# Selective scan and mixture of experts under adaptive layer norm, float32: the Newton step on rstd and the gates' low part from GpSimd to Vector, a seventh product with C on GpSimd

## The chip, the cores and the metric

One core of a Trainium2 chip runs the whole kernel in one launch. The metric is device time in microseconds. The engines are called as the profile calls them: PE (TensorE), DVE (VectorE), ACT (ScalarE), POOL (GpSimd) and SP (SyncE, which here only issues DMAs).

## The reference

The input x has 8 batches of 1024 tokens of 256 channels, in float32. Each batch has its own six modulation vectors, a product of `silu(c)` with `wmod`. Two blocks follow each other:

```python
mod = (_silu(L0_c) @ L0_wmod).reshape(L0_c.shape[0], 6, 1, -1)
sa, ca, ga, sb, cb, gb = (mod[:, 0], mod[:, 1], mod[:, 2], mod[:, 3], mod[:, 4], mod[:, 5])
h = _layernorm(x, axis=-1) * (1 + ca) + sa
x = x + ga * _L0_attn_ref(h, ...)      # selective scan
h = _layernorm(x, axis=-1) * (1 + cb) + sb
x = x + gb * _L0_ffn_ref(h, ...)       # mixture of 8 experts, 2 per token
```

In the first block, each of 256 channels has 16 states. `dt = softplus(...)` comes from two small projections of h, `a = exp(dt * A)`, `v = dt * u * B`, and each state runs the recurrence `h = a * h + v` along the 1024 tokens. The output is `y = sum over the 16 states of h * C`, plus `u * D`. In the second block a softmax over 8 experts picks the top two; their outputs are weighed by gates and added.

## The kernel before

**Tiling.** A stage is half a batch: 512 tokens, 256 channels as two tiles of 128 channels by 512 tokens. There are 16 stages, a first and a second half for each batch. The second half starts its scans from values kept from the first (tile `carry`).

**One stage.** For each of the 16 states n: SP loads the rows of B and C, spread over all partitions (`bb`, `cc`). POOL makes `v = du * bb` for both channel tiles at once (L1029, 128x1024). ACT makes `a` in PSUM (L1040), one per channel tile. DVE runs one scan per channel tile (L1051, a in PSUM, v in SBUF). The product with C goes either to DVE, two instructions of 128x512 into `hcD` (L1065), or to POOL, one of 128x1024 into `hs` (L1070). A string for each kind of stage, `C_ENG`, says which, state by state: D or P. PE adds the products up in PSUM, by transposes that accumulate into `y` (L1122). Before the states, POOL makes `du = dt * g` (L968) from ACT's softplus `dt` (L962).

**The back part of a stage** runs during the states of the next one: x + y on DVE (L1158), statistics of the layer norm (L786, L789), the factors of the norm, the norm itself on ACT (L831), transposes on PE (L862), a high and a low part of the result (`hi`, `lo`), the logits, the route (some fifteen small DVE steps, L1250 to L1271), the gates and their high and low parts (`gs`, L1297 and L1300), eight experts on PE (L1340), weighed by ACT (L1418) and summed by PE (L1428). POOL issues the DMA that adds the result to the output (L1501).

**The factors of the norm.** ACT guesses rstd with a logarithm and an exponential (L808 to L811). One Newton step then refines it: five small steps on the SBUF tile `ln` (128 x 8 in the middle stages, since the statistics of x two stages on are taken along), each using the result of the one before (L816 to L820, on POOL).

**Order.** No order is written out by hand. Each operation is given to a planner with its engine, a cost, and a due time `DUE[kind]`, one value per kind and phase; the phases are stage 0, stage 1, the middle stages 2 to 13, stage 14 and stage 15. The planner runs a model of the five engines, always takes the operation due first among those ready or soon ready (`PATIENCE` says how soon, per engine), and so fixes the order on every engine. `RINGS` gives the number of buffers per kind of tile: 4 of `v`, 3 of `hs`, 3 of `a`, 5 of `bb`, for instance. An operation that needs a buffer waits until all users of the one four (three, five) back have ended.

```python
def with_c(s, n):
    return ("hcD" if C_ENG[(0, 0, 2 - stages[s].first, 3, 3)[phase_of(s)]][n] == "D" else "hs", s, n)
```

So the first of the four strings of `C_ENG` is for stages 0 and 1, the second for the first halves among stages 2 to 13 (2, 4, ... 12), the third for their second halves, the fourth for stages 14 and 15.

Of the kernel before, what the change touches and what calls it, by code (L numbers as in the profile page):

```python
# [29 lines left out]
C_ENG = ("DDPDDPDDPDDPDDPD", "DPDDPDPDPDPDPDDD", "DPDPDPDPDPDPDPDD", "DDPDDPDDPDDPDDDD")  # L30
AHEAD = 1668.1
PATIENCE = {"ACT": 0.14, "DVE": 0.13, "PE": 0.25, "POOL": 0.5, "SP": 0.28}
# [5 lines left out]
    "load c": -2243.51,  # L38
    "load wmod0": -2004.07,
    "load wmod1": -1988.48,  # L40
    "load wmod2": -2.06,
    "load wmod3": -1957.81,
    "load W_x": -1.71,
    "load W_dt": -1965.24,
    "load b_dt": -116.61,
    "load A": -369.4,
    "load D": -1656.1,
    "load Wg": -357.62,
    "Wg hi": -1640.08,
    "Wg lo": -1616.04,  # L50
    "c^T": -414.35,
    "exp c": -1984.89,
    "1 + exp c": -351.35,
    "1 / c": -1644.2,
    "silu c": -1648.48,
    "mod1": -29.89,
    "mod1 out": -1640.92,
    "mod1 + 1": -57.77,
    "mod2": -97.07,
    "mod2 out": -2072.57,  # L60
    "mod3": -2117.64,
    "mod3 out": -1963.21,
    "mod3 + 1": -1953.8,
    "ga0": -437.02,
    "ga1": -460.54,
    "ga2": -73.86,
    "ga3": -2623.36,
    "gb0": -1953.35,
    "gb1": -357.52,
    "gb2": -461.1,  # L70
    "gb3": -27.31,
    "ga mod": -63.28,
    "ga mod D": 262.7,
    "1 / ga": -76.35,
    "gb^T": 279.89,
    "gb out": -406.31,
    "gb store": -483.98,
    "W_x^T": -3768.39,
    "W_x out": -436.84,
    "W_dt^T": -374.71,  # L80
    "W_dt out": -436.11,
    "exp A": -369.97,
    "-A": -74.32,
    "be rows": -2072.64,
    "be hi": -98.66,
    "be lo": -1963.34,
    "be": -55.72,
    "eps": -4332.43,
    "gates hi": (-235.79, -2460.72, -339.79, -149.99, -1797.16),
    "gates lo": (-24.1, -2044.84, -2133.06, -343.23, -3860.41),  # L90
    "load be": -15.49,
    "iw": -70.2,
    "load x": (-1989.96, -1978.86, -17.48, 8.4, -7.21),
    "stats1": (-2009.67, -1972.63, -69.27, -86.05, 47.99),
    "aggr1": (-1640.3, -1975.3, -1.3, -91.31, -2296.04),
    "before1": (-107.3, 986.06, -2961.9, -2961.25, -2977.69),
    "rstd1": (-359.36, 14.85, -2578.96, -2707.53, -2572.88),
    "norm1": (-24.76, -3800.78, 53.71, -15.89, -19.88),
    "trans1_0": (-2098.37, 28.07, -3664.64, -2478.96, -2711.13),
    "modg_0": (962.12, -427.57, -16.09, -2517.23, -444.87),  # L100
    "modD_0": (-1969.85, -43.93, -15.26, 0.47, -464.06),
    "trans1_1": (-2098.96, -16.51, -1646.42, -70.34, -17.88),
    "modg_1": (962.68, 28.65, -3869.23, -4.95, -390.32),
    "modD_1": (-16.02, -141.37, -3869.42, -2640.81, -526.1),
    "W_x / ga": (-2440.92, -1341.87, -50.77, -365.17, -1339.66),
    "proj": (-46.32, -3262.07, -1417.18, -7075.25, -1106.5),
    "rows": (-113.21, 892.07, -2147.14, -25.83, -373.01),
    "spill": (-1509.92, -46.65, -82.13, -108.28, -408.55),
    "dt0": (-2836.1, -86.93, -410.11, -472.19, -22.27),
    "softplus0": (8.96, -483.31, -563.94, -2696.95, -430.27),  # L110
    "dt1": (-2436.14, 985.9, -367.41, -1987.69, -75.38),
    "softplus1": (-3763.28, -2241.26, -2842.46, -2274.94, -367.03),
    "du": (-486.18, -2239.99, -70.63, -2154.13, -1629.08),
    "load B": (-1369.55, -17.6, -22.69, -296.42, -29.81),
    "load C": (-0.98, -16.67, 9.77, -2484.98, -15.04),
    "v": (-499.25, -85.1, -76.35, -47.8, 21.22),
    "a0": (-416.33, -341.56, -12.06, -392.16, -398.23),
    "a1": (-2633.56, -2630.9, -2268.36, -376.87, -2271.91),
    "scan0": (-345.29, -130, -84.13, -483.71, 835.51),
    "keep0": (-2622.16, -2801.29, -2480.02, -431.11, -2842.99),  # L120
    "C0": (-421.59, -408.48, -2258.73, -2296.35, -21.24),
    "scan1": (-350.22, -136.94, -86.02, -2760.06, -4.38),
    "keep1": (-2229.92, -335.27, -2547.2, -437.52, -439.8),
    "C1": (-414.5, -73.48, -2299.69, -2313.25, -19.25),
    "C": (-493.68, -127.22, -2167.24, -2223.87, 18.97),
    "y D": (19.24, -476.83, -54.5, -465.41, -8.25),
    "y": (-2254.19, -1637.88, -9.88, -1109.95, -3.56),
    "y C": (-473.82, -1635.95, -9.36, -7.82, 0.38),
    "load We": 4.3,
    "We hi": 992.95,  # L130
    "We lo": -499.19,
    "x + y": (-2642.38, -4495.38, -2303.57, -15.13, 893),
    "store x": (-2250.83, -2697.53, -2498.03, -14.55, -4714.94),
    "stats2": (-456.02, -1616.02, -2198.38, 0.86, -442.22),
    "aggr2": (-1761.59, -1623.66, -1485.56, 4.02, -32.11),
    "before2": (-53.78, -586.98, -7.88, 277.95, -2145.97),
    "rstd2": (-1659.97, -76.28, -71.01, -1965.28, -301.08),
    "norm2": (-15.76, -2440.99, -2156.75, 21.3, -62.97),
    "trans2_0": (-427.62, -2364.93, -1608.28, -17.84, 261.41),
    "hi0": (-2629.72, -4055.61, -4630.1, -3019.49, -2113.5),  # L140
    "mod2_0": (-343.91, -1615.01, -2238.87, -947.94, -35.03),
    "lo0": (-1317.6, -80.15, -2289.65, -464.16, 16.03),
    "trans2_1": (-3111.61, -1780.04, -10.03, -2604.76, 261.39),
    "hi1": (-2600.7, -738.55, -2256.02, 51.68, -2142.05),
    "mod2_1": (-359.16, -1823.24, -2242.34, -2256.16, 65.08),
    "lo1": (-2347.63, -3887.63, -77.67, -574.96, -1738.61),
    "logits^T": (-86.05, 0.71, -4.18, 0.12, 26.21),
    "logits out": (-2084.24, -89.2, -2470.09, -2118.52, -71.72),
    "logits": (-589.23, -70.63, -1938.4, -18.59, -408.58),
    "route": (-2625.88, -2360.01, -3907.92, -64.39, -2292.96),  # L150
    "gates": (-133.28, -75.36, -3858.04, -2448.11, -2203.07),
    "gates^T": (-2898.97, -1962.73, -2234.43, -4003.16, 6.19),
    "gates out": (-85.21, -9.58, -616.13, -18.22, -363.26),
    "biases": (-1642.72, -1.18, 6.14, 4.55, -932.33),
    "expert0": (-1632.13, -334.88, 2.48, 0.74, 28.86),
    "weigh0": (-2623.2, -2251.01, -2465.87, -2251.67, -3291.15),
    "sum0": (-1630.65, -2.35, 6.77, 2.59, 343.88),
    "gb": (-6.16, -2002.75, -2252.74, -1770.24, -2231.99),
    "turn": (13.97, 2.84, 5.77, -17.42, 288.49),
    "out": (-2240.75, -63.84, -406.3, -1777.56, -2456.12),  # L160
    "expert1": (-89.29, -20.09, 1.79, 275.85, 64.81),
    "weigh1": (-5.26, -122.87, -2272.08, -2165.17, -179.06),
    "sum1": (-5.22, -8.29, 3.93, 280.73, -101.5),
    "store": (-32.73, -46.88, -15.77, 11.83, -2124.92),
    "load gb": (-1904.24, -1904.24, -1904.24, -1904.24, -2839.22),
    "last bias": -92.62,
    "last": -2205.05,
    "last expert": 307.58,
    "last store": -16.76,
# [252 lines left out]
def kernel(  # L422
# [358 lines left out]
    def statistics(i, s, t, part, st, o):  # L781

        x, k0, tg, n_ = ("x", s), part[0], part[1] - part[0], str(i)

        def stats(k):
            nc.vector.bn_stats(new("st", st, [P, 2 * TG, 8])[:, o + k, 0:6], T[x][:, k0 + k, :])  # L786

        def aggr(k):
            nc.vector.bn_aggr(T[st][:, o + k, 6:8], T[st][:, o + k, 0:6])  # L789

        for k in range(tg):
            plan.add(
                "stats" + n_, "DVE", 0.33 if i == 2 else 0.39, t, lambda k=k: stats(k), r=[x + ((k0 + k) // 2,)],
                w=[st + (o + k,)], ring=("st", st),
            )
        for k in range(tg):
            plan.add("aggr" + n_, "DVE", 0.09, t, lambda k=k: aggr(k), w=[st + (o + k,)])

    def factors(i, t, st, ln, n):
# [13 lines left out]
        def newton():  # L813

            r, m, v, tt = row(0), row(1), row(2), nc.gpsimd.tensor_tensor
            tt(m, r, r, ALU.mult)  # L816
            tt(m, m, v, ALU.mult)
            nc.gpsimd.tensor_scalar(m, m, -0.5, 1.5, ALU.mult, ALU.add)
            tt(r, r, m, ALU.mult)
            tt(m, row(3), r, ALU.mult)  # L820
# [4 lines left out]
        plan.add("rstd" + n_, "POOL", 0.95 + 0.055 * n, t, newton, r=[st], w=[ln])  # L825
# [323 lines left out]
    def back(s, t, part):  # L1149
# [164 lines left out]
        for i in (0, 2):  # L1314
            plan.add("gates hi", "ACT", 0.18, t, lambda i=i: gates_hi(i), r=[G], w=[gs + (i,)], ring=("gs", gs))
# [247 lines left out]
```

## Time and profile before

| what | value |
|---|---|
| median of 3 runs | 1039.54 us (1039.06 to 1041.3) |
| the profiled execution: its time, its span | 1040.26 us, 1038.5 us |
| busy: PE, DVE, ACT, POOL | 928.7, 959.8, 845.7, 918.5 us |
| 255 v products on POOL (L1029) | 605.8 us, 2404 ns each |
| 96 C products on POOL (L1070) | 229.9 us, 2396 ns each |
| 320 C products on DVE (L1065) | 214.2 us, 684 ns each |
| 19 Newton steps of five on POOL (L816 to L820) | 0.20 us per instruction |
| 17 low parts of the gates on POOL (L1300) | 4.7 us, 279 ns each |
| granted TensorE clock, mean | 0.962 |

Durations are of one profiled execution. An instruction's duration runs from its start to its end, including time in which it has begun but is held up. Instructions that follow each other on DVE overlap a little, so what one costs its queue is the time from start to start: 0.61 us for a C product on DVE, for instance. Lines in the profile have the form: line, engine, operation, what it writes <- what it reads, shapes, count, then busy time and mean duration, then idle time before it and what ended most of that.

### The profile page before, as it was taken

How to read it: one execution, taken by the hardware profiler on the slowest of the kernel's cores; microseconds unless marked ns; L12 is line 12 of the kernel's file. 1: busy time of each engine (PE TensorE's matmuls, PEld its weight loads, DVE VectorE, ACT ScalarE, POOL GpSimd, SP SyncE). 2: the span in 40 equal slices, each digit the busy share in tenths (PEclk: the TensorE clock that was granted, in tenths of full speed). 3: DMA queues.
4: the chain of work that ended last, by engine and by line, in shares of the span. 5: the costliest groups of instructions: out<-in, count | busy, mean ns of one | idle time of the engine just before them, and what ended most of it. 6: DMA issues, size and time to landing. Idle time of an engine off the chain costs nothing. (4 is left out here: it accounts for less than half of the span.)

```text
span 1038.5 us, 17114 instructions
## 1 busy us (share of the span) xinstructions
PE 928.7 (89%) x5525; PEld 739.9 (71%) x5525; DVE 959.8 (92%) x1488; ACT 845.7 (81%) x1845; POOL 918.5 (88%) x515
## 2 busy tenths in 40 slices
PE   6656798798899989999999989999998998999998
PEld 4444676586676868687777868688686867778886
DVE  3798999999999999999999999999999998999947
ACT  5855678889699988988899988988898986988661
POOL 4999879999999999999999999999999997988600
PEclk9657998899899999999999999999999999999999
DMA  6556327375655647475665737475575637656102
GB/s 203 185 182 219 122 88 234 96 209 147 194 157 156 208 108 211 113 217 155 166 221 146 219 85 212 123 209 175 138 240 128 221 67 204 169 148 198 39 6 46
DMA packets 103865, 165.20 MB, mean 159 GB/s; under 512 B 10160, under 2 KB 37216, under 8 KB 103776
## 3 DMA queue, kind: packets, MB, share of 16 engines
q1 hardware_dynamic: 95728, 156.22, 49.4%
q0 software_dynamic: 8048, 7.89, 5.1%
q8 instruction: 44, 0.72, 0.3%
q14 instruction: 45, 0.37, 0.1%
HBM read 146.76 MB, written 17.31 MB: 158 GB/s over the span
## 5 line engine op out<-in xcount | busy, mean ns | idle before, releaser
L1029 POOL TENSOR_TENSOR v<-du,bb 128x1024 f32<-128x1024 f32 x255 | 605.8, 2404 | 17.8 <-DMA bb<-bcd 11.7
L1040 ACT ACTIVATE a<-dt,negA 128x512 f32<-128x512 f32 x512 | 348.5, 697 | 52.9 <-DVE hcD L1065 33.0
L1070 POOL TENSOR_TENSOR hs<-hs,cc 128x1024 f32<-128x1024 f32 x96 | 229.9, 2396 | 17.1 <-issue 8.7
L1065 DVE TENSOR_TENSOR hcD<-a,cc 128x512 f32<-128x512 f32 x320 | 214.2, 684 | 13.9 <-ACT carry L1057 7.0
L1418 ACT ACTIVATE wt<-pe,G 128x256 f32<-128x256 f32 x480 | 201.6, 474 | 18.5 <-PE pe L1340 16.8
L1122 PE MATMUL y<-ident,hcD 128*128 128x128 f32 x1280 | 183.3, 285 | 34.8 <-DVE hcD L1065 34.6
L1051 DVE TENSOR_TENSOR_SCAN a<-a,v 128x512 f32<-128x512 f32 x166 | 195.6, 1213 | 8.5 <-POOL v L1029 4.8
L1051 DVE TENSOR_TENSOR_SCAN a<-a,carry,v 128x512 f32<-128x512 f32 x154 | 196.2, 1277 | 1.4 <-POOL v L1029 0.7
L1122 PEld LDWEIGHTS y<-ident,hcD 128*128 128x128 f32 x1280 | 153.8, 147 | 58.0 <-DVE hcD L1065 44.2
L1340 PE MATMUL pe<-we_hi,hi 128*128 128x512 f32 x512 | 179.2, 431 | 7.3 <-ACT wt L1418 4.3
L1340 PE MATMUL pe<-we_lo,hi 128*128 128x512 f32 x512 | 160.7, 395 | 0.0
L1340 PE MATMUL pe<-we_hi,lo 128*128 128x512 f32 x512 | 160.5, 395 | 0.0
L1428 PE MATMUL ma<-ident,wt 128*128 128x128 f32 x960 | 135.8, 275 | 1.2 <-ACT wt L1418 1.2
L1122 PE MATMUL y<-ident,hs 128*128 128x128 f32 x768 | 109.7, 285 | 24.2 <-POOL hs L1070 23.9
L1051 DVE TENSOR_TENSOR_SCAN hs<-a,carry,v 128x512 f32<-128x512 f32 x102 | 125.2, 1266 | 0.0
L1428 PEld LDWEIGHTS ma<-ident,wt 128*128 128x128 f32 x960 | 112.1, 141 | 16.2 <-ACT wt L1418 2.0
L1122 PEld LDWEIGHTS y<-ident,hs 128*128 128x128 f32 x768 | 92.1, 146 | 37.4 <-POOL hs L1070 31.1
L1340 PEld LDWEIGHTS pe<-we_lo,hi 128*128 128x128 f32 x512 | 96.3, 188 | 22.9
L1340 PEld LDWEIGHTS pe<-we_hi,lo 128*128 128x128 f32 x512 | 96.1, 188 | 23.1
L1051 DVE TENSOR_TENSOR_SCAN hs<-a,v 128x512 f32<-128x512 f32 x90 | 106.3, 1208 | 0.0
L1340 PEld LDWEIGHTS pe<-we_hi,hi 128*128 128x128 f32 x512 | 81.5, 190 | 25.6 <-ACT wt L1418 9.2
L831 ACT ACTIVATE xn<-x,ln 128x256 f32<-128x256 f32 x128 | 72.0, 599 | 3.0 <-POOL ln L820 3.0
(134 smaller groups left out, 936.9 us busy)
## 6 DMA issues: line engine op xcount, KB each, us to landing
bb<-bcd SPq DMA_DIRECT2D x256, 256.0 KB, 5.5
cc<-bcd SPq DMA_DIRECT2D x256, 256.0 KB, 5.2
x<-in_L_attn_u_dram SPq DMA_DIRECT2D x16, 512.0 KB, 3.7
out_dram<-x SPq DMA_DIRECT2D x15, 512.0 KB, 3.4
out_dram<-of POOLq DMA_DIRECT2D x15, 512.0 KB, 12.1
wf<-in_L_ffn_We_dram SPq DMA_DIRECT2D x8, 256.0 KB, 4.1
wm<-in_L_wmod_dram SPq DMA_DIRECT2D x2, 512.0 KB
bcd<-xd SPq DMA_DIRECT2D x32, 32.0 KB, 1.6
```

Source lines behind the costliest of these rows:

```text
L831: nc.scalar.activation(new("xn", xn, [P, TG, D])[:, k, :], T[x][:, k0 + k, :], AF.Identity, bias=T[ln][:, 1, o + k : o + k + 1], scale=T[l ...
L1029: nc.gpsimd.tensor_tensor(new("v", v, [P, DC, CL])[:, :, :cl], T["du", s][:, :, :cl], both(T[bb][:, :cl]), ALU.mult,)
L1040: nc.scalar.activation(new("a", a + (j,), [P, CL])[:, :cl], T["dt", s][:, j, :cl], AF.Exp, scale=negA[:, j, n : n + 1],)
L1051: nc.vector.tensor_tensor_scan(part(j), T[a + (j,)][:, :cl], T[v][:, j, :cl], init, ALU.mult, ALU.add)
L1065: nc.vector.tensor_tensor(new("hcD", hc, [P, DC, CL])[:, j, :cl], part(j), T[cc][:, :cl], ALU.mult)
L1070: nc.gpsimd.tensor_tensor(o, o, both(T[cc][:, :cl]), ALU.mult)
L1122: nc.tensor.matmul(new("y", y, [P, 2, D])[:, k % 2, j * P : (j + 1) * P], T[src][:, j, k * P : (k + 1) * P], ident, is_transpose=True, sta ...
L1340: nc.tensor.matmul(pe, T[v][:, j, k * P : (k + 1) * P], w[:, j, 2 * q : 2 * q + 2, :].rearrange("p e d -> p (e d)"), start=n == 0, stop=n ...
L1418: nc.scalar.activation(new("wt", wt, [P, 2, D])[:, i, :], T["pe", s, part, q, k][:, i * D : (i + 1) * D], AF.Copy, scale=T[G][:, k, e : e ...
L1428: nc.tensor.matmul(o[:, j, (k % 2) * P : (k % 2 + 1) * P], T["wt", s, q, k][:, i, j * P : (j + 1) * P], ident, is_transpose=True, start=Fa ...
```

## The change

The five Newton steps go from POOL to DVE, and so does the low part of the gates. The second string of `C_ENG` changes from six products with C on POOL to seven; the third had seven already. Two orders on PE are fixed by added dependencies: the transposes of the first norm and the D part of y go in the order of the stages. Some costs that the planner is given are changed, as are `AHEAD`, `PATIENCE` and all of `DUE`, so that the order on every engine is planned anew.

```diff
-C_ENG = ("DDPDDPDDPDDPDDPD", "DPDDPDPDPDPDPDDD", "DPDPDPDPDPDPDPDD", "DDPDDPDDPDDPDDDD")
-AHEAD = 1668.1
-PATIENCE = {"ACT": 0.14, "DVE": 0.13, "PE": 0.25, "POOL": 0.5, "SP": 0.28}
+C_ENG = ("DDPDDPDDPDDPDDPD", "DPDPDPDPDPDPDPDD", "DPDPDPDPDPDPDPDD", "DDPDDPDDPDDPDDDD")
+AHEAD = 2063.23
+PATIENCE = {"ACT": 0.15, "DVE": 0.22, "PE": 0.22, "POOL": 0.21, "SP": 1.43}
...
         def newton():
 
-            r, m, v, tt = row(0), row(1), row(2), nc.gpsimd.tensor_tensor
+            r, m, v, tt = row(0), row(1), row(2), nc.vector.tensor_tensor
             tt(m, r, r, ALU.mult)
             tt(m, m, v, ALU.mult)
-            nc.gpsimd.tensor_scalar(m, m, -0.5, 1.5, ALU.mult, ALU.add)
+            nc.vector.tensor_scalar(m, m, -0.5, 1.5, ALU.mult, ALU.add)
             tt(r, r, m, ALU.mult)
             tt(m, row(3), r, ALU.mult)
...
-        plan.add("rstd" + n_, "POOL", 0.95 + 0.055 * n, t, newton, r=[st], w=[ln])
+        plan.add("rstd" + n_, "DVE", 0.4, t, newton, r=[st], w=[ln])
...
         plan.add(
-            f"trans{i}_{j}", "PE", (0.13 if i == 1 else 0.11) * tg, t, f, r=[xn + (k,) for k in range(tg)], w=[pt],
+            f"trans{i}_{j}", "PE", (0.15 if i == 1 else 0.12) * tg, t, f, r=[xn + (k,) for k in range(tg)] + ([("t1", s - 1)] if i == 1 and s else []),
+            w=[pt] + ([("t1", s, j)] if i == 1 else []),
...
             plan.add(
-                "y D", "PE", 0.22 * len(tiles), t, lambda: more(gd), r=[gd], w=[y], ring=("y", y)
+                "y D", "PE", 0.22 * len(tiles), t, lambda: more(gd), r=[gd] + ([("yd", s - 1)] if s else []),
+                w=[y, ("yd", s)], ring=("y", y)
             )
...
         def gates_lo():
-            nc.gpsimd.tensor_tensor(
+            nc.vector.tensor_tensor(
                 T[gs][:, :tg, 1], T[G][:, :tg], T[gs][:, :tg, 0].bitcast(F32), ALU.subtract
             )
...
-        plan.add("gates lo", "POOL", 0.22, t, gates_lo, r=[G, gs + (0,)], w=[gs + (1,)], ring=("gs", gs))
+        plan.add("gates lo", "DVE", 0.1, t, gates_lo, r=[G, gs + (0,)], w=[gs + (1,)], ring=("gs", gs))
...
```

In the new order, as the built program has it, Newton stands on DVE in stages 3 to 13 between the two scans of state 4 (in second halves behind the first C product of that state too), and the low part of the gates between the two scans of state 11 in nearly all of these stages. On POOL the order from a stage's start is v0, v1, v2, v3, v4 and C1 (in either order), v5, the store of an earlier stage's result, v6, C3, v7, v8.

## The prediction, made before the changed kernel ran

> **What bounds the kernel now.** I read the page's busy times first, then windows, to see in which stretch which engine is full.
>
> ```profile
> PE 928.7 (89%) x5525; PEld 739.9 (71%) x5525; DVE 959.8 (92%) x1488; ACT 845.7 (81%) x1845; POOL 918.5 (88%) x515
> ```
>
> ```profile
> 195.00:845.00 650.00, 609.48 (x3758) 486.97 (x3756) 632.72 (x947) 573.96 (x1246) 633.34 (x336) 0.99 0.59 170
> 845.00:975.00 130.00, 124.64 (x757) 99.78 (x755) 119.36 (x173) 109.56 (x244) 110.28 (x60) 1.00 0.54 151
> 975.00:1038.50 63.50, 58.32 (x324) 47.21 (x322) 41.94 (x99) 27.86 (x74) 8.68 (x16) 0.98 0.16 28
> ```
>
> The columns after the length are PE, PEld, DVE, ACT and POOL busy. From 195 to 845 us (stages 3 to 13, about 59.1 us each) DVE and POOL are both 97% busy, PE 94%, ACT 88%. After 845 us DVE has 8% to spare and PE sets the pace. So an addition to DVE's own queue costs nearly its full length in the middle stages, and little in the last two. The rows that fill the two engines:
>
> ```profile
> L1029 POOL TENSOR_TENSOR v<-du,bb 128x1024 f32<-128x1024 f32 x255 | 605.8, 2404 | 17.8 <-DMA bb<-bcd 11.7
> L1070 POOL TENSOR_TENSOR hs<-hs,cc 128x1024 f32<-128x1024 f32 x96 | 229.9, 2396 | 17.1 <-issue 8.7
> L1065 DVE TENSOR_TENSOR hcD<-a,cc 128x512 f32<-128x512 f32 x320 | 214.2, 684 | 13.9 <-ACT carry L1057 7.0
> ```
>
> Queued behind each other, a POOL product costs 2.36 us from start to start (four v in 9.45 us at 443.09), a product with C on DVE 0.61, a scan 1.12 (1.19 with a carried start).
>
> POOL's timeline at the start of stage 7 shows how a stage begins and what the Newton step costs there:
>
> ```profile
> 440.62 2.40 POOL L968 TENSOR_TENSOR du<-dt,g 128x1024 f32<-128x1024 f32 x1 [0.45 <-ACT dt L962]
> 443.09 9.45 POOL L1029 TENSOR_TENSOR v<-du,bb 128x1024 f32<-128x1024 f32 x4
> ...
> 459.53 0.19 POOL L816 TENSOR_TENSOR ln<-ln 128x8 f32<-128x8 f32 x1
> ...
> 460.66 0.20 POOL L820 TENSOR_TENSOR ln<-ln 128x8 f32<-128x8 f32 x1
> 460.88 2.39 POOL L1070 TENSOR_TENSOR hs<-hs,cc 128x1024 f32<-128x1024 f32 x1
> ```
>
> POOL waits for dt, makes du, then v0; v0 ends at 445.5 and DVE's first scan of the stage starts at 445.51. ACT writes dt after the last a of the stage before, and a waits for banks that the scans free. So at each stage's start POOL's lead over DVE is set back to zero, whatever POOL had gained. DVE waits for little else:
>
> ```profile
> DVE hcD L1065 <- ACT carry L1057: 4.1, 16, 0.5
> DVE a L1051 <- POOL v L1029: 1.7, 8, 0.5
> DVE a L1051 <- ACT a L1040: 1.6, 4, 0.4
> ```
>
> These are DVE's waits from 195 to 845 us. No DVE instruction of the middle stages reads two tensors from SBUF: a, y, pt and pl lie in PSUM. In the setup a few do, and there DVE's timeline, and POOL's beside it, show something that bears on this change:
>
> ```profile
> 32.02 1.28 DVE L653 TENSOR_SCALAR tmp<-modT 128x16 f32<-128x16 f32 x1
> 33.33 0.17 DVE L654 TENSOR_SCALAR tmp<-tmp 128x16 f32<-128x16 f32 x1
> 33.42 1.25 DVE L655 SCALAR_TENSOR_TENSOR tmp<-modT 128x16 f32<-128x16 f32 x1
> 48.94 0.83 DVE L656 SCALAR_TENSOR_TENSOR modT<-tmp 128x16 f32<-128x16 f32 x1
> ```
>
> ```profile
> 32.00 1.27 POOL L968 TENSOR_TENSOR du<-dt,g 128x512 f32<-128x512 f32 x1
> 33.35 1.28 POOL L1035 TENSOR_TENSOR v<-du,bb 128x512 f32<-128x512 f32 x1
> 47.36 2.37 POOL L1070 TENSOR_TENSOR hs<-hs,cc 128x1024 f32<-128x1024 f32 x1
> ```
>
> At 14.7 to 15.2 us, with POOL idle, the same three instructions (L653, L655, L656) took 0.14, 0.17 and 0.17 us. Here each ends within 0.04 us of the end of the POOL product beside it (33.30 against 33.27, 34.66 against 34.63, 49.77 against 49.73). They waited for POOL, and DVE's queue stood behind them. Only L654, issued in a gap of 0.08 us between two POOL products, got through.
>
> **The Newton step on DVE: arithmetic.** It has four tensor_tensor and one tensor_scalar per group on the tile ln, all in SBUF, each needing the one before. Such small dependent steps run 0.20 to 0.23 us from start to start on DVE (L655 to L656 0.20, the route's steps 0.21 to 0.23): 5 x 0.21 = 1.05 us a stage. POOL is relieved of 460.88 - 459.53 = 1.35 us a stage.
>
> **Its waits for POOL.** Newton's tensor_tensor is nearest to L655 and L656, which read two SBUF tensors as it does, its tensor_scalar to L653. And at 13.44 us a POOL step of 0.20 us lasted 0.44, up to 0.07 us after the end of a DVE tensor_tensor on two SBUF tensors (13.40 to 13.81). So I take it that all five wait when they meet a POOL product, and follow the queues. In the new order of stages 3 to 13 Newton stands behind the first scan of state 4 (in odd stages behind a C product too). POOL's queue from v0 is nine products and a store's descriptors: v1 to v5 with C1 among them, the store, v6, C3, v7; then v8, which needs a v buffer that state 4's scans free, and half of these stand behind Newton. So POOL runs on to the end of v7 and no further.
> Odd stages, from v0's end: DVE needs 17.1 us to Newton (nine scans 1.19 to 1.36, five C products 0.61, residual 1.2, statistics 1.6); POOL has v5 done at 14.1, the store at 14.9 (its row at 498.64 lasts 1.26 us, and the next product starts 0.40 before its end), v6 at 17.3, C3 at 19.6, v7 at 22.0. One Newton step goes at each end: the first at 17.3, the second at 19.6, the third at 22.0, and the last two meet an idle POOL. Newton ends at 22.4 instead of 18.15: 4.3 us of waiting. Should two steps pass at each end, the last still stands until about 22. Even stages: DVE is there at 16.2, scans being shorter, and the wait is 5.2. Mean 4.75 us. The ends: nothing, if POOL is idle or such small steps slip through; 5 x 2.36 = 11.8 if each meets a full product, which the blocked v8 excludes. With DVE or POOL shifted by one product it is 2.4 or 7.1, my ends.
> The Trainium skill, "SBUF — State Buffer", section "Who interferes with whom", speaks against this change: a DVE instruction with two SBUF inputs, or a tensor_scalar in a two-port mode, contends with a GpSimd instruction that reads SBUF, and whichever is later is blocked wholly. The rows show it for tensor_scalar and scalar_tensor_tensor; for the four tensor_tensor waiting on POOL only the page says it. By the page all five steps wait, as in my sum; if only Newton's tensor_scalar waited, it would be about 1.2 us a stage.
>
> **Gates' low part.** One DVE step with two SBUF inputs (G and gs) between the two scans of state 11: 0.1 us plus a wait between 0 (POOL blocked before C11) and 2.36. I take 0.9, a little under half a product. POOL loses 0.25.
>
> **The seventh C product.** In six first halves (stages 2 to 12) two DVE products go, 2 x 0.61 = 1.2 us, 0.6 per stage on average, and POOL gets 2.36. Per pair of stages POOL changes by 2.36 - 2 x (1.35 + 0.25) = -0.8. Being no longer the later one, it gives nothing back.
> The skill's "GPSIMD Engine Reference", section "4.1 Engine selection", sends elementwise work to VectorE, at about twice the speed. The rows give 0.21 us against 0.28 per Newton step; by the page's factor Newton would cost DVE some 0.7 us of the 1.35 instead of 1.05, 4 us less in all.
>
> **The fixed orders and the new plan.** No instruction is added on PE or SP (1825 and 583 listed rows in both). After the last y product PE has the same work in both orders (144 expert matmuls and small ones, 41 us), so the tail stays. The store on POOL moves from ahead of du, where POOL waited for dt anyway (0.45 us), to behind v5; it falls in the time in which POOL runs ahead, and delays v6, which is in the sum. ACT, PE and SP have work queued behind DVE's stall, but ACT has 12% of idle time and PE 6%, and a longer stage gives them more. For setup and stage 1, where POOL leads by 3 to 11 us, I count nothing and allow 5 us either way.
>
> **The sum.** Per stage on DVE: 1.05 + 4.75 (Newton) + 1.0 (gates) - 0.6 (C) = 6.2. DVE's idle time in stage 7 is 0.3 + 1.0 = 1.3 us; I let 0.7 of it absorb some: 5.5 us. Over stages 2 to 13: 12 x 5.5 = 66. The profiled execution took 1040.26 us (span 1038.5): 1106; the median lies 0.7 lower: 1105.5.
>
> **Rivals.**
> *Faster: POOL sets the stage, and the small steps slip through.* The place is du and v0, where DVE's first scan waits for POOL. With no waits at the port, POOL's 0.4 us a stage is the gain: 12 x 0.4 = 5, 1034.5 us. It decides if Newton, waits included, stays within the 1.3 us of DVE's idle time per stage. For it: POOL is as full as DVE, and L654 passed. Against it: three of four instructions waited, and POOL has a product queued in nearly every instant.
> *DVE's arithmetic alone.* No waits, but DVE fuller by 1.05 + 0.1 - 0.6 = 0.55 us a stage: 12 x 0.55 = 6.6 at most, less what idle time absorbs, 1039.5 to 1046.
> *One product only.* POOL is further ahead than I reckon and blocked soon: each Newton waits some 1.2 us and the gates nothing. Per stage 1.05 + 1.2 + 0.1 - 0.6 = 1.75: 21 us, 1060. Against it: the reset of the lead at each stage's start.
>
> **How the numbers follow.** My forecast has 0.78. Its own range: a wait of 2.4 makes 3.15 a stage (+38), a wait of 7.1 with a full product at the gates (1.45 more) 9.3 (+112); both at once in every stage is unlikely, so +32 to +100 with the setup's 5: 1072 to 1140. One product only has 0.09, arithmetic alone 0.06, faster 0.07. Differences under 0.2%, 2 us, can't be told from no change. The range 1058 to 1140 takes in the third rival and leaves out some 0.18. Faster 0.07; same 0.03, half of arithmetic alone; slower 0.90.
>
> **What would show it.** In the profile after, the ln rows on DVE have mean durations near 1 us, not 0.2, and end with POOL products; DVE's busy time grows, since waiting counts as busy (L653's 1.28); POOL falls to about 90% in the middle; stages last some 64.5 us. If the ln rows take 0.2 us each, the forecast is wrong at its root; if they wait but stages last 60, other idle time absorbed it.

## The result: 1141.6 us, 9.7% slower, and the profile after

The changed kernel takes 1141.63 us (median of 4 runs, 1140.0 to 1142.41); the kernel before takes 1040.42 beside it (4 runs). The ratio is 1.0971, 95% interval 1.0949 to 1.0992. The direction and most of the mechanism were as forecast, the size was not: 101 us instead of 66, just above the end of the range. The profiled execution's span is 1139.6 us (1038.5 before).

The page's busy times, and the windows from 195 to 845 us and over stage 15 (columns after the length: PE, PEld, DVE, ACT, POOL, granted clock, DMA share, GB/s):

```profile
PE 963.1 (85%) x5525; PEld 773.7 (68%) x5525; DVE 1053.1 (92%) x1588; ACT 845.7 (74%) x1839; POOL 910.9 (80%) x409
```

```profile
195.00:845.00 650.00, 562.74 (x3319) 455.65 (x3318) 626.02 (x894) 511.35 (x1107) 566.36 (x247) 0.93 0.52 151
1019.60:1088.00 68.40, 59.90 (x362) 50.50 (x361) 65.29 (x79) 44.95 (x96) 47.19 (x21) 0.93 0.43 118
```

DVE's busy time grew by 93 us for 100 small instructions: most of that is standing. In the middle POOL fell from 97% to 87% busy, ACT from 88% to 79%, PE from 94% to 87%. The granted clock of PE fell with it, from 0.99 to 0.93; how much a slower PE adds to the loss was not tested by itself. The groups with the new work on DVE, and POOL's products:

```profile
L816 DVE TENSOR_TENSOR ln<-ln 128x8 f32<-128x8 f32 (+2 forms) x19 | 58.1, 3057 | 1.8 <-ACT ln L809 1.8
L1302 DVE TENSOR_TENSOR gs<-G,gs 128x32 fp32r<-128x32 f32 (+1 forms) x17 | 15.8, 927 | 0.3 <-ACT gs L1299 0.3
L817 DVE TENSOR_TENSOR ln<-ln 128x8 f32<-128x8 f32 (+2 forms) x19 | 15.2, 802 | 2.0 <-ACT ln L810 0.2
L818 DVE TENSOR_SCALAR ln<-ln 128x8 f32<-128x8 f32 (+2 forms) x19 | 5.4, 282 | 0.7
L820 DVE TENSOR_TENSOR ln<-ln 128x8 f32<-128x8 f32 (+2 forms) x19 | 3.2, 166 | 1.9
```

```profile
L1030 POOL TENSOR_TENSOR v<-du,bb 128x1024 f32<-128x1024 f32 x255 | 612.0, 2430 | 62.0 <-DVE a L1052 37.9
```

The same operation on the same tile takes 3057 ns where it stands first (L816) and 166 ns where it stands last (L820). The last figure is its cost, the rest is waiting, booked as busy. And POOL now stands idle 62 us before its v products (17.8 before), 37.9 of them for DVE's scans to free a v buffer.

Stage 7 shows one such wait, DVE first, POOL below:

```profile
504.17 4.98 DVE L816 TENSOR_TENSOR ln<-ln 128x8 f32<-128x8 f32 x1
509.25 0.17 DVE L817 TENSOR_TENSOR ln<-ln 128x8 f32<-128x8 f32 x1
509.45 0.17 DVE L818 TENSOR_SCALAR ln<-ln 128x8 f32<-128x8 f32 x1
509.66 0.17 DVE L819 TENSOR_TENSOR ln<-ln 128x8 f32<-128x8 f32 x1
509.93 0.17 DVE L820 TENSOR_TENSOR ln<-ln 128x8 f32<-128x8 f32 x1
```

```profile
500.84 1.22 POOL L1503 DMA_DIRECT2D out_dram<-of  x1
501.65 2.83 POOL L1030 TENSOR_TENSOR v<-du,bb 128x1024 f32<-128x1024 f32 x1
504.00 2.81 POOL L1071 TENSOR_TENSOR hs<-hs,cc 128x1024 f32<-128x1024 f32 x1
506.35 2.77 POOL L1030 TENSOR_TENSOR v<-du,bb 128x1024 f32<-128x1024 f32 x1
511.43 2.36 POOL L1030 TENSOR_TENSOR v<-du,bb 128x1024 f32<-128x1024 f32 x1 [2.32 <-DVE a L1052]
```

L816 meets v6 and stands until 509.15. Two products end meanwhile, v6 at 504.48 and C3 at 506.81, and it gets in at neither; it ends 0.03 us after v7 (509.12), when POOL has nothing left that it could start. v8, the last row, waits 2.32 us for a scan behind Newton. In stage 4 the store's descriptors come 12 us before Newton (295.19), with idle time of POOL in between, and there it goes as the prediction had it, one step at each end:

```profile
307.23 0.59 DVE L816 TENSOR_TENSOR ln<-ln 128x8 f32<-128x8 f32 x1
307.85 2.31 DVE L817 TENSOR_TENSOR ln<-ln 128x8 f32<-128x8 f32 x1
310.19 2.27 DVE L818 TENSOR_SCALAR ln<-ln 128x8 f32<-128x8 f32 x1
312.50 0.17 DVE L819 TENSOR_TENSOR ln<-ln 128x8 f32<-128x8 f32 x1
```

```profile
305.38 2.42 POOL L1030 TENSOR_TENSOR v<-du,bb 128x1024 f32<-128x1024 f32 x1
307.71 2.42 POOL L1071 TENSOR_TENSOR hs<-hs,cc 128x1024 f32<-128x1024 f32 x1
310.06 2.38 POOL L1030 TENSOR_TENSOR v<-du,bb 128x1024 f32<-128x1024 f32 x1
```

The POOL products end at 307.80, 310.13 and 312.44; L816, L817 and L818 end 0.02 to 0.03 us behind them. L818, the tensor_scalar, waits too, with one SBUF input.

**Where the 101 us lie**, by cutting each span at the first scan of every stage (sums of the trace's rows on DVE, an instruction's overlap with the one before it taken off):

| us, before to after | before | after | difference | prediction |
|---|---|---|---|---|
| start, stages 0 and 1 | 155.0 | 156.9 | +1.9 | 0 |
| stages 2 to 13: Newton | 0 | 67.9 | +67.9 | +69.6 |
| gates' low part | 0 | 9.4 | +9.4 | +12 |
| C products | 146.1 | 138.5 | -7.6 | -7.2 |
| scans | 446.6 | 446.4 | -0.2 | 0 |
| other work of DVE | 93.0 | 99.0 | +6.0 | 0 |
| DVE idle | 20.9 | 32.2 | +11.3 | -8.4 |
| stage 14 | 63.7 | 69.4 | +5.7 | 0 |
| stage 15 and what follows it | 113.2 | 120.0 | +6.8 | 0 |

Other work grew mostly by its place: the new order does two sums x + y and some of the statistics in stages 2 and 3 that were done in stage 1 (4.9 of the 6.0 us are there without any wait too, in e1 below). In stages 0 and 1 Newton and the gates take 6.3 us, and DVE's idle time falls by 3.7.

### The profile page after: what moved, and what is told of

It is laid out like the page before. It is cut to its first block, busy times and chain, and to the rows that moved or that the text cites. A ratio compares the mean times of both kernels' runs of the same rounds, so it can differ in the third digit from the quotient of the medians.

```text
span 1139.6 us, 17170 instructions
## 1 busy us (share of the span) xinstructions
PE 963.1 (85%) x5525; PEld 773.7 (68%) x5525; DVE 1053.1 (92%) x1588; ACT 845.7 (74%) x1839; POOL 910.9 (80%) x409
## 5 line engine op out<-in xcount | busy, mean ns | idle before, releaser
L1030 POOL TENSOR_TENSOR v<-du,bb 128x1024 f32<-128x1024 f32 x255 | 612.0, 2430 | 62.0 <-DVE a L1052 37.9
L1071 POOL TENSOR_TENSOR hs<-hs,cc 128x1024 f32<-128x1024 f32 x102 | 246.7, 2418 | 59.0 <-ACT carry L1062 15.8
L1123 PE MATMUL y<-ident,hcD 128*128 128x128 f32 x1232 | 190.0, 300 | 90.0 <-DVE hcD L1066 89.7
L1066 DVE TENSOR_TENSOR hcD<-a,cc 128x512 f32<-128x512 f32 x308 | 206.0, 682 | 13.4 <-ACT carry L1058 8.1
L1052 DVE TENSOR_TENSOR_SCAN a<-a,v 128x512 f32<-128x512 f32 x154 | 181.7, 1210 | 15.3 <-POOL v L1036 11.9
L1342 PE MATMUL pe<-we_hi,hi 128*128 128x512 f32 x512 | 186.3, 446 | 4.8 <-ACT wt L1420 2.1
L1430 PE MATMUL ma<-ident,wt 128*128 128x128 f32 x960 | 141.9, 281 | 0.0
L1123 PE MATMUL y<-ident,hs 128*128 128x128 f32 x816 | 122.1, 289 | 9.7 <-POOL hs L1071 9.7
L1052 DVE TENSOR_TENSOR_SCAN hs<-a,v 128x512 f32<-128x512 f32 x102 | 121.6, 1207 | 2.0 <-ACT a L1041 1.4
L1123 PEld LDWEIGHTS y<-ident,hs 128*128 128x128 f32 x816 | 101.9, 150 | 16.6 <-POOL hs L1071 12.7
```

Of the source, the lines that this page charges most:

```text
L1030: nc.gpsimd.tensor_tensor(new("v", v, [P, DC, CL])[:, :, :cl], T["du", s][:, :, :cl], both(T[bb][:, :cl]), ALU.mult,)
L1052: nc.vector.tensor_tensor_scan(part(j), T[a + (j,)][:, :cl], T[v][:, j, :cl], init, ALU.mult, ALU.add)
L1066: nc.vector.tensor_tensor(new("hcD", hc, [P, DC, CL])[:, j, :cl], part(j), T[cc][:, :cl], ALU.mult)
L1071: nc.gpsimd.tensor_tensor(o, o, both(T[cc][:, :cl]), ALU.mult)
L1123: nc.tensor.matmul(new("y", y, [P, 2, D])[:, k % 2, j * P : (j + 1) * P], T[src][:, j, k * P : (k + 1) * P], ident, is_transpose=True, sta ...
L1342: nc.tensor.matmul(pe, T[v][:, j, k * P : (k + 1) * P], w[:, j, 2 * q : 2 * q + 2, :].rearrange("p e d -> p (e d)"), start=n == 0, stop=n ...
```

## Experiments

Ratios are to the kernel before on the same chip, with 95% intervals. Four groups each have runs of the kernel before of their own: e1, e2, e3, e6; e4, f1, f2, f4; e5, g1, f5, f3; and h1, h2.

### e1: the same order, but no second SBUF input

```diff
-            tt(m, r, r, ALU.mult)
...
-            tt(m, row(3), r, ALU.mult)
+            r, m, inv = row(0), row(1), nc.vector.reciprocal
+            inv(m, r); inv(m, m); inv(m, m); inv(r, m); inv(m, r)
...
-                T[gs][:, :tg, 1], T[G][:, :tg], T[gs][:, :tg, 0].bitcast(F32), ALU.subtract
+                T[gs][:, :tg, 1], view(1), T[gs][:, :tg, 0].bitcast(F32), ALU.subtract
```

`view(1)` lies in PSUM, the rows of `ln` in SBUF.

> The changed kernel in its own order on every engine; only the operands of the moved DVE steps differ: the five Newton steps are reciprocals of the same 128x8 rows (one SBUF input each, rstd unrefined and the norm's bias wrong), and the gates' low part subtracts from a PSUM tile (pl) instead of G. Theory 1 (the waits for POOL, and everything that follows from them, are the whole loss): no step waits, each ln row takes 0.2 us or less, and the time falls to about 1047 us (1040.4 + 12 x 0.55). Theory 2 (the new order itself costs the idle time of the middle stages and the 12 us of stages 14 and 15): 1060 to 1077. Theory 3 (it is the number of steps on a full DVE, not their operands): 1140, unchanged.

Measured: 1044.32 us, ratio 1.0034 (1.0022 to 1.0045). The first three of the five steps at Newton's place in stage 7, the gates' low parts of the whole run, and the window from 195 to 845 us:

```profile
463.84 0.19 DVE L816 RECIPROCAL ln<-ln 128x8 f32<-128x8 f32 x1
464.06 0.20 DVE L817 RECIPROCAL ln<-ln 128x8 f32<-128x8 f32 x1
464.30 0.20 DVE L818 RECIPROCAL ln<-ln 128x8 f32<-128x8 f32 x1
```

```profile
L1302 DVE TENSOR_TENSOR gs<-pl,gs 128x32 fp32r<-128x32 f32 (+1 forms) x17 | 2.9, 170 | 0.3 <-ACT gs L1299 0.3
```

```profile
195.00:845.00 650.00, 612.24 (x3772) 488.52 (x3771) 632.28 (x1000) 575.61 (x1246) 632.06 (x276) 1.00 0.60 171
```

As many steps in the same order at the same place; 0.20 us each, POOL back at 97%, the granted clock at 1.00. So 97 of the 101 us come from steps with two SBUF inputs (and the tensor_scalar) beside a full POOL, and from what follows their waits. For the gates the operation is the same and one operand lies elsewhere (170 ns against 927); Newton's operations differ too, and e6 below settles that. What is left of the change is no gain either: 4 us slower.

### e2: one step instead of five

```diff
-            tt(m, r, r, ALU.mult)
...
-            tt(m, row(3), r, ALU.mult)
+            tt(row(1), row(3), row(0), ALU.mult)
```

> The changed kernel in its own order with four of the five Newton steps left out (rstd stays the guess; only the bias product is made, one tensor_tensor with two SBUF inputs). If one step gets through at each end of a POOL product, as the prediction's working had it, a single step waits about 1 us instead of 4.75: about 12 x 4.6 = 55 us less, 1086. If the first step waits until POOL has nothing more at hand, whatever the number of steps, only the arithmetic of four steps goes: 15 x 0.85 = 13 us less, 1129.

Measured: 1106.54 us, ratio 1.0637 (1.0607 to 1.0667), between the two expectations. DVE's row in stage 7:

```profile
491.87 4.99 DVE L816 TENSOR_TENSOR ln<-ln 128x8 f32<-128x8 f32 x1
```

A single step stands as long as the first of five did; in stages 5 to 13 it took 4.98 to 6.27 us. So there the wait doesn't depend on the number of steps, and "one step at each end" is wrong for them. The time fell by 35 us, more than the 13 of the second expectation. In stages 2 to 4 steps do go one by one: of the 16.7 us by which Newton's sum fell in stages 2 to 13, 10.2 lie there, the rest is about the arithmetic of four steps. Idle time fell by 7.1, the gates' waits grew from 9.4 to 17.0. And stage 15 is 11.5 us shorter (68.4 to 56.9): Newton's single step there did not wait, nor did the gates' one.

### e3 and e6: planned anew

e3 puts Newton and the gates' low part back on POOL in the planner too; e6 keeps them on DVE, in four steps, but has ACT write the guess and the negated mean into PSUM.

```diff
-        plan.add("rstd" + n_, "DVE", 0.4, t, newton, r=[st], w=[ln])
+        plan.add("rstd" + n_, "POOL", 0.95 + 0.055 * n, t, newton, r=[st], w=[ln])    # e3
+        plan.add("rstd" + n_, "DVE", 0.85, t, newton, r=[st, pn], w=[ln])             # e6
...
+            nc.scalar.activation(pr(0), row(2), AF.Exp, scale=-0.5)                   # e6
...
+            tt(m, pr(0), row(2), ALU.mult)                                            # e6
+            stt(m, m, -0.5, pr(0), ALU.mult, ALU.mult)
+            stt(r, m, 1.5, pr(0), ALU.add, ALU.mult)
+            tt(m, pr(3), r, ALU.mult)
```

> The changed kernel with Newton and the gates' low part back on POOL at their old planner costs; seven C products on POOL in both halves, the fixed orders and the new due times stay (the planner orders anew from these). Theory 1 (the waits are the whole loss): 1035 to 1048. Theory 2 (the new plan costs some 20 to 30 us by itself): 1060 to 1075.

> The change in a form without a second SBUF input: ACT writes the guess and the negative mean into a PSUM bank of ring psm, Newton is four DVE steps with one PSUM and at most one SBUF input, and the gates are also written to pl, from which the low part is taken. Everything is computed; the planner orders anew with the changed kernel's due times. Theory 1: the moved steps cost only 12 x 0.4 us of DVE arithmetic, less what POOL's relief gives; 1036 to 1052, the upper end if the held bank delays PE. Theory 2: 1055 to 1080. Theory 3: above 1100.

Measured: 1113.38 (1.0711, 1.068 to 1.0743) and 1127.87 (1.0832, 1.0808 to 1.0855). e3 is above both its expectations, e6 lies where theory 3 had it by its number, but neither time tests a theory: the planner, given other costs with the same due times, wrote another order, and that order alone is slow. None of the moved steps stands behind a POOL product in either, but DVE stands idle 69.9 and 77.0 us in stages 2 to 13, against 20.9 before (e3's stages last 56 to 74 us).

e6's rows are of use all the same:

```profile
L822 DVE TENSOR_TENSOR ln<-pn,ln 128x8 f32<-128x8 f32 x14 | 2.1, 154 | 0.0
L823 DVE SCALAR_TENSOR_TENSOR ln<-ln,pn 128x8 f32<-128x8 f32 x14 | 2.3, 162 | 0.5
```

These are a tensor_tensor, the operation that waited in the change, and a scalar_tensor_tensor, the one that waited in the setup before (L655), with one of the two inputs in PSUM. 30 of the 38 tensor_tensor rows of Newton lie wholly within a POOL product, and none lasted over 0.17 us. So it is the place of the second input that counts, not the operation. From here on every experiment keeps a planned order as it is and changes only what is issued in it.

### e4: does the norm, late behind Newton, make DVE idle?

ACT's norm waits for Newton:

```profile
ACT xn L831 <- DVE ln L820: 73.4, 16, 6.4
```

Theory A: through norm, transposes and `lo` this comes back to DVE as idle time. Theory B: DVE's held queue alone does it. In e4 Newton writes rows that nobody reads, so the norm doesn't wait.

```diff
-            tt(m, r, r, ALU.mult)
+            o = new("nw", ("nw",) + ln[1:], [P, 4, 2 * TG])
+            q, b_ = o[:, 0, :n], o[:, 1, :n]
+            tt(q, r, r, ALU.mult)
...
-                bias=T[ln][:, 1, o + k : o + k + 1], scale=T[ln][:, 0, o + k : o + k + 1],
+                bias=T[ln][:, 3, o + k : o + k + 1], scale=T[ln][:, 0, o + k : o + k + 1],
```

> The changed kernel in its own order, with the five Newton steps on DVE as they are but writing to rows of their own that nobody reads; the norm on ACT reads ACT's own guess and negative mean instead (rstd unrefined, bias wrong). DVE's waits for POOL stay. Theory A (the idle time that DVE gained in the middle stages, 11 us where the prediction let 8 be absorbed, comes from ACT, whose norm stands in its queue until Newton ends, with the a's behind it): the ln rows stay near 6 us a stage, DVE's idle time falls by 8 to 12 us, the run takes about 1129 us. Theory B (DVE's own stall leaves a's and v's unmade, whatever ACT waits for): within 3 us of 1141.

Measured: 1139.92, ratio 1.096 (1.0937 to 1.0984); DVE's idle time in stages 4 to 13 is 25.6 us against 26.7, where theory A had it fall by 8 to 12. Theory A falls.

### f1, f2, f4: the parts of the change one by one

f1: the order of before, Newton and gates issued on DVE. f2: the new order, both issued on POOL. f4: the order of before, POOL's Newton cut to its last product.

```diff
-            r, m, v, tt = row(0), row(1), row(2), nc.gpsimd.tensor_tensor    # f1, on before
+            r, m, v, tt = row(0), row(1), row(2), nc.vector.tensor_tensor
...
-            r, m, v, tt = row(0), row(1), row(2), nc.vector.tensor_tensor    # f2, on after
+            r, m, v, tt = row(0), row(1), row(2), nc.gpsimd.tensor_tensor
```

> The kernel before in its own order on every engine, six C products, with only Newton and the gates' low part issued on DVE instead of POOL, at the place that the order gives them. If the waits for POOL come with any order: stages of some 64 to 67 us, 1105 to 1145. If it was the new order that put Newton where POOL has three products at hand: 1045 to 1070.

> The changed kernel in its own order on every engine, with Newton and the gates' low part issued on POOL at the places that the order gives them; seven C products on POOL stay. No DVE step waits for POOL. POOL carries 1.6 us more per stage than with these steps on DVE: 1044.3 (the one-input run in the same order) + up to 12 x 1.6 - 12 x 1.0 of DVE's relief: 1044 to 1058. Theory 2, the new order bad by itself: above 1060.

> The kernel before in its own order, with four of Newton's five steps on POOL left out (rstd stays ACT's guess; the bias product stays). POOL is relieved of 4 x 0.28 = 1.1 us a stage. If POOL sets the middle stages: 12 x 1.1 less, 1027. If DVE sets them as much as POOL, or du waits for dt anyway: 1034 to 1040.

Measured: f1 1125.07 (1.0815, 1.0775 to 1.0855), f2 1064.0 (1.0228, 1.0206 to 1.0249), f4 1042.69 (1.0019, 1.0001 to 1.0037). The waits come with the old order as well (f1: Newton 53.1, gates 15.9 us in stages 2 to 13). These stages became 71.3 us longer, and DVE's idle time in them went from 20.9 to 23.4: there idle time absorbs nothing of the waits, but they make next to no new idle time either. The new order with POOL still loaded (f2) is 2.3% slower, above what was expected: DVE then stands idle 42.3 us in stages 2 to 13, against 20.9 before. The order is not slow by itself, as e1 shows; with its seventh C product it needs the relief of POOL. And relief for POOL alone (f4) brings nothing, where both expectations had some gain; that fits "set back to zero at each stage's start".

### e5: hold DVE's queue without any port

e1, with 26 aggregations of a constant tile behind each Newton of the second norm.

```diff
+            if i == 2:
+                jk = new("jk", ("jk",) + ln[1:], [P, 8])
+                for _ in range(26):
+                    nc.vector.bn_stats(jk[:, 0:6], ident)
```

> The one-input run (changed order, no waits for POOL) with some 5 us of DVE work put where each Newton step of the second norm stands: 26 statistics of the 128x128 identity into a tile that nobody reads. So DVE's queue is held as long as Newton held it, but by its own work and not by POOL. Theory B1 (a queue held for 5 us is enough to make DVE idle more afterwards, since a's and transposes stand behind each other on ACT and PE): idle time of DVE in stages 4 to 13 near 26 us, as in the changed kernel, not 17; total 1044 + 15 x 5 + 10 = 1129. Theory B2 (it comes from POOL running ahead or from the port): idle near 17, 1119.

Measured: 1192.91, ratio 1.1463 (1.1421 to 1.1504). The hold was 8.46 us a stage, not the 5 meant (the 26 stand 0.33 us apart from start to start), so the totals of the two theories can't be compared with the time. DVE's idle time in stages 4 to 13 is 34.1 us, of which 8.4 are the gaps between the 26 themselves, part of the hold; the other 25.7 are what theory B1 has. Idle gaps of over 0.12 us: 16.4 us, against 16.1 in the change, 8.0 in e1 and 10.3 before, and at the same places: 2.16 us where an `a` scan follows an `hs` scan (2.15 in the change), 3.8 us before `lo`, which waits for `pt` (2.4 in the change, none in e1). A longer hold did not make more of them. So in the new order holding DVE's queue is enough to make idle time later, whatever holds it. It is not so everywhere: f1, in the old order, spends 55.8 us on Newton and the gates in the same stages (65.0 in the change), Newton's 7.2 us at a time in the odd ones, and has 10.5 us of such gaps. Whether the order or the place of the hold makes the difference, and through which engine, stays open.

### g1: no store in POOL's queue

```diff
-            nc.gpsimd.dma_start(out=orow, in_=T[of][:, :tg], accum_op=ALU.add)
+            pass
```

> The changed kernel in its own order with the 15 stores on POOL left out (the expert part never reaches the output). In the changed kernel POOL's products overlap by 0.3 to 0.57 us behind a store, and no waiting DVE step got in at such an end; where they overlap by under 0.1 us most got in. If the store is what makes POOL's products follow so closely, Newton's steps go in one at each product end again, the first waits 0 to 2.3 us and not 5 to 6; Newton's total per stage falls only by the store's 0.9 us, since POOL still runs on to v8: 1125 to 1131. If the store has no part in it, single waits of 5 us stay.

Measured: 1102.01 (two runs, 1095.4 and 1108.6), ratio 1.0589 (1.0506 to 1.0672). Stage 7, DVE, then POOL:

```profile
493.22 1.43 DVE L816 TENSOR_TENSOR ln<-ln 128x8 f32<-128x8 f32 x1
494.75 2.21 DVE L817 TENSOR_TENSOR ln<-ln 128x8 f32<-128x8 f32 x1
497.00 0.17 DVE L818 TENSOR_SCALAR ln<-ln 128x8 f32<-128x8 f32 x1
```

```profile
492.25 2.38 POOL L1071 TENSOR_TENSOR hs<-hs,cc 128x1024 f32<-128x1024 f32 x1
494.59 2.35 POOL L1030 TENSOR_TENSOR v<-du,bb 128x1024 f32<-128x1024 f32 x1
```

With the store gone one step goes at each end again (494.63 and 496.94), as in stage 4. Newton falls from 67.9 to 43.4 us in stages 2 to 13, and the time by 40 us where 11 to 17 were expected: even stages get several steps through a gap of some 0.6 us in POOL's queue. How steps get in is thus tied to what precedes POOL's products.

### f5 and f3: one part without waits; the old order without waits

f5: e1's reciprocals, but the gates' low part as in the change. f3: e1's steps on DVE in the order of before, with six C products.

```diff
-            tt(m, r, r, ALU.mult)      # f5 on after, f3 on before (there from nc.gpsimd)
...
+            inv(m, r); inv(m, m); inv(m, m); inv(r, m); inv(m, r)
```

> The changed kernel in its own order with Newton as reciprocals (one SBUF input, rstd unrefined, bias wrong) and the gates' low part as in the change (two SBUF inputs). What is left of the loss is the gates' part. If the parts add: 1044 + the 9 us of gates waits seen in the changed kernel: 1053. With POOL less far ahead than behind a long Newton wait, each gates step may wait more, up to a product: 1044 + 17 x 1.2 = 1064.

> The kernel before in its own order, six C products, with Newton as reciprocals (one SBUF input, rstd unrefined, bias wrong) and the gates' low part from PSUM, both issued on DVE at the places that the order gives them. DVE gets 1.15 us a stage, POOL loses 1.6, nobody waits at the port. If POOL sets the middle stages, 1025 to 1035; if both are tied through du and dt, as the run with one Newton step on POOL suggests, 1040 to 1054.

Measured: f5 1069.98 (1.0285, 1.0258 to 1.0312), f3 1056.6 (1.0157, 1.0128 to 1.0185). Both lie above what was expected (1053 to 1064, and 1040 to 1054). In f5 the 17 low parts alone cost 26 us: their waits in stages 2 to 13 are 20.8 us, not 9.4, which fits a POOL that is fuller once Newton no longer stalls the stage. So the parts don't add up. f3 shows what DVE arithmetic costs: 11.9 us of moved rows in stages 2 to 13, 1.0 a stage, made these 10.0 us longer. e1 is 12 us better than f3: the seventh C product (7.5 us less of DVE's rows in stages 2 to 13) and the new order (5.0 us of other work more in these stages, and stages 0, 1 and 15 with what follows 12.0 us shorter) pay for most of the moved work, once nothing waits. What each of the two is worth was not separated.

### h1 and h2: two SBUF rows read as one input

A tensor_reduce that multiplies along an axis reads two rows of `ln` as one strided input. h1 has only the last product in that form, without the refinement; h2 has the whole Newton step in four of them, for which ACT writes two more rows. In both the gates' low part reads G from a copy in PSUM.

```diff
+            red = nc.vector.tensor_reduce
+            red(row(4), pick(0, 3, 1), AX.X, ALU.mult)     # r * r * (-v / 2)
+            red(row(6), pick(1, 5, 3), AX.X, ALU.mult)
+            red(row(0), pick(5, 7, 1), AX.X, ALU.add)      # + 1.5 r
+            red(row(1), pick(0, 4, 3), AX.X, ALU.mult)     # alone in h1
```

> The changed kernel in its own order; Newton's refinement is left out (rstd stays ACT's guess) and the bias product is one tensor_reduce with multiply over the two rows, which has a single SBUF input; the gates are also written to pl by a second DVE step, and the low part is taken from there. No step waits for POOL. Per stage DVE has 0.2 us of Newton instead of 1.05 and 0.2 us more for the gates: 0.65 us less than the one-input run. If DVE's time counts in full: 1044.3 - 13 x 0.65 = 1036. If POOL, through du and dt, sets the pace once the waits are gone: 1041 to 1045.

> The same, with the whole Newton step: four tensor_reduce (multiply three times, add once) over rows of ln, one SBUF input each; ACT writes two rows more (the guess once more, and 1.5 times it). Everything is computed. DVE has 0.85 us of Newton and 0.2 for the gates' copy, as much as in the one-input run; ACT has 0.4 us more per stage. If only DVE counts: 1044. If ACT's two steps, which stand before the norm, count too: up to 1050. Waits at the port, if tensor_reduce had them after all: above 1090.

h2's rows in stage 7:

```profile
465.23 0.17 DVE L823 TENSOR_REDUCE ln<-ln 128x8 f32<-128x24 f32 x1
465.43 0.17 DVE L824 TENSOR_REDUCE ln<-ln 128x8 f32<-128x16 f32 x1
465.64 0.17 DVE L825 TENSOR_REDUCE ln<-ln 128x8 f32<-128x16 f32 x1
465.91 0.17 DVE L826 TENSOR_REDUCE ln<-ln 128x8 f32<-128x16 f32 x1
```

Measured: h2 1041.63 (12 runs), ratio 0.9996 (0.998 to 1.0013): the change's whole computation in the change's order, with no wait, equals the kernel before. h1 1031.64 (6 runs), ratio 0.9915 (0.9895 to 0.9935), the fastest of all, for less computed; the old kernel without the refinement (f4) took 1042.69. h1 is 4 us below the lower of its two expectations, h2 2 us below. Against e1, h1 is 12.7 us faster; of the 10.5 us between the profiled executions 6.9 lie in stages 2 to 13, where DVE's rows sum to 7.3 us less: there DVE's time counts nearly in full.

## Why the prediction was right in kind and too low

- **Newton's arithmetic** (1.05 us a stage): held. e1's steps are 0.22 to 0.24 us apart, h2's 0.20 to 0.27.
- **Newton's wait**: the size held, one link didn't. Newton took 67.9 us in stages 2 to 13 against 69.6 reckoned; in stage 7 it began 17.3 us after the first scan (17.1 reckoned), v7 ended at 22.3 (22.0), Newton at 23.3 (22.4). "One Newton step goes at each end" holds in stage 4 and fails in stages 5 to 13 (e2). The sum survived since it followed POOL's queue to where a missing buffer stops it, and the prediction said that the last step stands until then however many pass. That it came so near is in part luck, since the stages differ from it both ways: with the arithmetic 5.35 us were reckoned for odd stages and 6.25 for even ones, and Newton lasted 3.3 to 5.6 in stages 2 to 4, 5.9 in odd stages from 5 on, 7.0 to 7.4 in even ones. The text's "mean durations near 1 us" for all five rows is wrong with it: L816 has 3.06, L820 0.17.
- **Gates** (12 reckoned, 9.4 measured) and **C** (-7.2 and -7.6): held, the gates in their sum alone: 4.1 of the 9.4 us are one stage (3).
- **"I let 0.7 of it absorb some"**: the step that failed. DVE's idle time did not shrink by 8.4 us, it grew by 11.3, an error of 20 of the 35 us that the forecast lacks. Most of the 18.5 us of idle time in stages 4 to 13 before is no slack: 8.2 us are gaps under 0.12 us between DVE's own instructions, 3.7 us waits for ACT's carry copy. Both are there in the change too (10.6 and 3.3 us), however long DVE stood before. f1 shows the same without the new order: 69 us of Newton and gates, and idle time 2.5 us up. In the new order a hold makes new idle time besides (e5); why there and not in f1 stays open.
- **Stages 14 and 15 at nothing** ("DVE has 8% to spare and PE sets the pace"): failed as well, 12.5 us. The window of 130 us averaged two cases: DVE was 90% busy in stage 14 (57.43 of 63.7 us), but not in stage 15. That stage of before by itself, from the same view:

```profile
925.00:988.00 63.00, 62.56 (x400) 52.93 (x398) 61.18 (x85) 49.62 (x107) 47.40 (x27) 1.00 0.43 118
```

  DVE was 97% busy there, beside a PE at 99%. In the change Newton and the gates take 9.1 us of it (0.9 in e1), 5.5 us of other rows and C products have gone elsewhere, and its last scan ends 68.4 us after the start of its first, not 63.4 (57.2 in e1). In stage 14 Newton and the gates take 3.4 us. What follows the last scan grew by 1.8 us (49.8 to 51.6), near to the nothing that the prediction had.
- **Moved work**: 6.0 us in stages 2 to 13 that the prediction did not count. Stages 0 and 1, for which it allowed 5 us either way, are 1.9 us longer.
- Of the rivals, "DVE's arithmetic alone" (1039.5 to 1046) is what e1 and h2 measured with the waits taken away (1044.3, 1041.6). "Faster" would have needed less on DVE as well (h1).
- The Trainium skill, "SBUF — State Buffer", section "Who interferes with whom": that a tensor_tensor with two SBUF inputs waits, which only the page had, is now shown by rows of each of the four (L816 and L817 in the change, L819 with 2.26 us in f1, L820 with 2.18 us in g1), and the choice of all five steps over 1.2 us a stage was right. Following the rule of "GPSIMD Engine Reference", section "4.1 Engine selection" (elementwise work to VectorE), came with a loss of 9.7% here where the steps read two SBUF inputs; read as one input (h2) the change cost nothing and gained nothing.

## What to carry to other kernels

Before a small step with two SBUF inputs goes to DVE, look at what POOL has queued at that place: the price can be POOL's queue up to where it stops, not the step's 0.2 us; another form of the same step (one input in PSUM, two rows read as one strided input) takes the price away. Don't let a full engine's idle time absorb an addition before you know what the gaps are, and read a window by single stages before you call it slack. To test a planned kernel, keep its order and change what is issued in it: a plan made anew is another kernel.

## What the runs showed of the hardware beyond what was expected

- A waiting DVE step does not get in at every end of a POOL product. Where POOL's next product had started 0.29 to 0.57 us before the last one ended (the three products behind the store's descriptors in stage 7: 501.65 + 2.83 against 504.00, and so on), it got in 0 of 41 times in the change, e2 and f5; with an overlap of 0.12 us or less 20 of 27 times in the same runs, and 18 of 21 in the run without stores. That the overlap is the cause, rather than something that comes with it, was not tried by itself.
- The store's descriptors on POOL take 1.22 us, but the next product starts 0.81 us after their start (500.84 to 501.65), and this early start is handed on from product to product (2.83, 2.81 and 2.77 us long, 2.35 us from start to start).
- The reciprocals, tensor_reduce and bn_stats put in Newton's place on DVE never waited for POOL (at most 0.20, 0.18 and 0.30 us), nor did a tensor_tensor or scalar_tensor_tensor with one of its inputs in PSUM (e6, 0.17 us); the tensor_scalar did, with its one input in SBUF (L818, 2.27 us in stage 4). A tensor_reduce over two rows of one SBUF tile took 0.17 us beside a POOL at 97%.
